# Moving PSUM additions, weight steps, turned weights and one projection in a chained attention and RWKV kernel

## The chip, the cores and the metric

The kernel runs on one core of a Trainium2 chip. The metric is the device time of one execution in microseconds (us). The engines are TensorE (PE), VectorE (DVE), ScalarE (ACT), GpSimd (POOL) and SyncE (SP), which issues the DMAs.

## The reference

Input `x` has 8 sequences of 112 tokens with 512 channels; the context `ctx` has 8 sequences of 375 tokens with 512 channels. All is float32. Four layers follow one another:

```python
x = x + alpha * softmax(x@w_q.T @ (ctx@w_k.T).T / sqrt(512)) @ (ctx@w_v.T) @ w_o.T     # L0
for layer in (L1, L2):                                  # RWKV, state taken from ctx
    xa = layer_norm(x);  sx = shifted(xa) - xa
    m  = tanh((xa + sx*maa_x) @ maa_w1) @ maa_w2        # five mixes w, k, v, r, g
    xw, xk, xv, xr, xg = xa + sx * (maa + m)
    w = exp(-exp(time_decay + tanh(xw@d1) @ d2))
    r, k, v, g = xr@Wr.T, xk@Wk.T, xv@Wv.T, silu(xg@Wg.T)
    for t in range(112):                                # 32 heads, states of 16 x 16
        a = k[t][:, None] * v[t][None, :]
        y[t] = r[t] @ (u*a + s);  s = a + w[t][:, None] * s
    x  = x + (group_norm(y) * g) @ Wo.T
    xc = layer_norm(x);  sxc = shifted(xc) - xc
    x  = x + sigmoid((xc+sxc*fr)@Wfr.T) * (square(relu((xc+sxc*fk)@Wfk.T)) @ Wfv.T)
for i in (1, 2):                                        # L3, 16 heads of 128
    q, k, v = norm(x)@wq+bq, ctx@wk+bk, ctx@wv+bv       # and one bias row for k and v
    x = x + softmax(q @ k.T / sqrt(128)) @ v @ wo + bo
x = x + gelu(norm(x) @ w_fc1 + b_fc1) @ w_fc2 + b_fc2
```

## The kernel before

**Layout.** Channels lie on the 128 partitions in 4 chunks (`NC`); tokens lie along the free axis, 896 in all, mostly handled in two halves (`h`) of 448.

**A generator beside the layers.** The values of both attentions of L3, and a few of its keys, do not depend on `x`. The generator `values()` makes them while the RWKV layers run. Each `fill(n)` in a layer's code takes it n products on. Its work is 51 units: four sets of weights with 12 units of values (`wv`) each, and a last one with 3 units of keys (`wk`). A unit is a block product in the manner of Strassen with seven products, `k1, k6, k7, k2, k8` and, one product each into the next unit's time, `k5` and `k9` (`last_two`, L893). A product of values is two matmuls of 128x512 (four records in the trace), and an engine then empties the PSUM bank; two banks, `mm0` and `mm1`, take turns. ACT copies `k1`, `k6`, `k7` (L956) and `k8` (L973). For `k2`, ACT copies (L966) and GpSimd adds to an earlier result in SBUF (L967). For `k5` and `k9`, DVE adds from PSUM (L898, L902). A finished tile is stored to DRAM (`store`) on SP's queue; context tiles `cv` come on the same queue, four ahead.

**Weights between sets.** The seven weight tiles of a set are sums of raw weights. `relay` changes them one at a time: it yields the name of the product after which the next step may run, and `after(what)`, called behind each product, runs it. A step is a DMA (`raw`) on SP or a sum on GpSimd (L814 and its neighbours). This runs at 490 to 520 us, 1115 to 1150 and 1342 to 1362. The change from the second to the third set loads all anew (`weights`) in the first channel mix.

**A RWKV layer** first turns its weights `Wg` and `Wv` to another order of columns: for each of the 16 tiles of 128x128, ACT copies it out (L407) and GpSimd copies it back in the new order (L408), by a buffer of two. Of the first layer this happens in L0, of the second in the first layer's channel mix. Then for each half `h`, `mixes` makes the five mixes (DVE adds the two-input products to `sx`, L447, and `xa`, L450; GpSimd does it for three of the five), with `fill(fills[4 + c])` after each chunk c. While `mixes(1, ...)` runs, `fill` takes the pieces of `projections(0, ...)`, so its numbers say how many of these pieces come between which chunks. A piece of projection r is 16 matmuls.

**Time mix.** Per layer, 64 steps in an order written out by hand (`manual_schedule`): `kv` = `vp` times `k` on DVE (L675, result in PSUM), one product of values, ACT copies the next step's `vp` into PSUM (`led`, L576 and L577) from `vj`, which a DMA has broadcast; DVE scans `decay` and `kv` to `st` (L679); GpSimd multiplies `st` by `r` to `rs` (L683, six buffers); a second product of values in 14 of 16 steps; and TensorE sums four `rs` at a time once six are waiting. Pieces of the group norm of the chunk before stand at the end of steps: among them a square on ACT and reciprocals on DVE (L609).

**The rest.** The channel mix scales on DVE (`xk`, `xr`, L725) the differences `sxc` that GpSimd makes (L350, L351). The attentions of L3 run from 1513 us on.

Of the kernel before, what the change touches and what calls it, by code (L numbers as in the profile page):

```python
# [29 lines left out]
P = 128  # L30
# [59 lines left out]
def turned(ap):  # L90

    return ap.rearrange("p (h q r) -> p q h r", h=HB, q=4)
# [16 lines left out]
def tile_kernel(ctx: ExitStack, tc: tile.TileContext, d: dict, out: bass.AP):  # L109
# [21 lines left out]

    ident = const.tile([P, P], F32, name="ident")
    make_identity(nc, ident)
    mean_c = const.tile([P, P], F32, name="mean_c")
# [81 lines left out]
    def layer0():  # L216
# [3 lines left out]
        with (  # L220
# [3 lines left out]
            tc.tile_pool(name="a0s", bufs=2, space=PSUM) as ps2,  # L224
        ):
            w_q, w_k = weight("L0_xattn_w_q"), weight("L0_xattn_w_k")
            nc.sync.dma_start(x, d["xT"])
# [143 lines left out]
    def time_mix_inputs(n, pre, names, ones_t, first, k, v, r, g, decay, rows):  # L371
# [7 lines left out]
        with (  # L379
# [22 lines left out]
            for f in "gv":  # L402
                for o in range(NC):
                    for c in range(NC):
                        w = ws[f][:, c, o * P : (o + 1) * P]
                        t = work.tile([P, NH], F32, tag="e", name=f"turn{f}{n}_{o}_{c}")[:, :P]
                        nc.scalar.copy(t, w)  # L407
                        nc.gpsimd.tensor_copy(w.rearrange("p (q h r) -> p q h r", q=4, h=HB), turned(t))  # L408

# [48 lines left out]
            def projections(h, xw, xg):  # L458

                p = mm(ps, f"ps_d{n}_{h}")[:, :NH]  # L460
                for c in range(NC):
                    nc.tensor.matmul(p, d1[:, c, :], xw[:, c, :], start=c == 0, stop=c == NC - 1)
                td = one.tile([P, NH], F32, tag="td", name=f"td{n}_{h}")
                nc.scalar.activation(td, p, AF.Tanh)
# [66 lines left out]
            values_filler, filler = filler, pieces  # L531
            following = projections(1, *mixes(1, (2, 1, 2, 1, 1, 0, 0, 0)))
            filler = values_filler
# [227 lines left out]
    def rwkv_layers():  # L761
        with tc.tile_pool(name="rc", bufs=1) as one:
# [5 lines left out]
            with tc.tile_pool(name="rs", bufs=1) as setup:  # L768
                heads = setup.tile([P, P + P + HS - 1], F32, name="heads")
                nc.sync.dma_start(heads, d["heads"])  # L770

                nc.vector.tensor_copy(ones_t.rearrange("p (q h r) -> p q h r", q=4, h=HB), turned(heads[:, :P]))
                same = setup.tile([P, P], F32, name="same")
                for q in range(4):
                    nc.sync.dma_start(same[32 * q : 32 * (q + 1)], turned_rows(d["heads"][:, :P], q))
                nc.scalar.mul(mean_h.rearrange("p (q h r) -> p q h r", q=4, h=HB), turned(same), 1.0 / HS)
                nc.vector.tensor_sub(less_mean_h, ident, mean_h)

                for r in range(4):
                    at = P + HS - 1 - 4 * r  # L780
                    nc.vector.tensor_copy(pick[:, r], heads[:, at : at + 16 * HB - 3 : 4])
# [6 lines left out]
    def values():  # L788
# [31 lines left out]
        def relay(at, old, new):  # L820
# [5 lines left out]
            for y, o, k in ((a11, 0, 0), (a21, 1, 0), (a22, 1, 1)):  # L826
                raw(y, at, o, k)
            yield "k1"
            nc.gpsimd.tensor_sub(old["k1"], a11, a21)
# [7 lines left out]
            raw(old["k8"], at, 1, 1)  # L837
            new.update(k1=a11, k6=old["k6"], k7=old["k1"], k2=old["k7"], k8=old["k8"], k5=old["k9"], k9=old["k2"])
            yield "k5"
# [41 lines left out]
        def store(y, u, o, j):  # L881
# [10 lines left out]
            else:  # L892
                nc.sync.dma_start(where[:, t], y)  # L893

        def last_two(u, f, u2, u3, s, at):
            p = bank(u, f, f"k5_{u}")
            product(p, block(at), s["k5"])
            nc.vector.tensor_add(u3, p, u3)  # L898
            store(u3, u, 1, 1)
            yield "k5"  # L900
            product(p, block(at + 2), s["k9"], start=False)
            nc.vector.tensor_add(u2, p, u2)  # L902
            store(u2, u, 0, 1)
            yield "k9"
# [11 lines left out]
        yield  # L916
        before, steps, following = iter(()), iter(()), None

        def after(what):
            nonlocal following  # L920
            if what == following:
                following = next(steps, None)
# [8 lines left out]
        for u, (at, unit) in enumerate(units):  # L931
# [9 lines left out]
            if unit == UNITS - 2 and at != 1:  # L941
                new = {}
                steps = relay(at + 1, s, new)
                ready = next(steps)
            elif unit == UNITS - 1 and at != 1:
                following = ready
            if unit % 3 == 0:
                for gr in groups:
# [14 lines left out]
            product(p, block(base + 5), s["k2"])  # L963

            y = shaped(pool.tile([P, C], F32, tag="k2", name=f"k2_{u}"), f)
            nc.scalar.copy(y, p)  # L966
            nc.gpsimd.tensor_add(p1, y, p1)  # L967
            store(p1, u, 0, 0)
# [114 lines left out]

    def attention(i, h_in, work, kv, ps, ps2, keep, mlp_norm):
        nonlocal filler
# [220 lines left out]
    def layer3():  # L1306
        with (
# [5 lines left out]
        ):  # L1313
            h_in = keep.tile([P, NC, N], F32, name="h_in")
            with tc.tile_pool(name="t3s", bufs=1, space=PSUM) as ps2:
                def mlp_norm(h, bank):
# [13 lines left out]
                for i in (1, 2):  # L1330
                    attention(i, h_in, work, kv, ps, ps2, keep, mlp_norm)
            mlp(h_in, work, ps, keep, shared["t_mlp"])
# [86 lines left out]
```

## Time and profile before

| quantity | us |
|---|---|
| median of 3 runs (lowest to highest) | 3005.23 (2998.66 to 3009.64) |
| the profiled execution, own time | 3006.6 |
| its span | 3004.8 |
| TensorE busy | 2874.8 |
| DVE busy | 1713.4 |
| ACT busy | 862.4 |
| GpSimd busy | 732.9 |
| first time mix | 364.5 to 631 |
| second time mix | 1003 to 1281 |
| attentions of L3 and MLP | 1513 to the end |

In rows of the profile the first item is the line of the kernel, then engine, operation, and tiles written and read. A count follows an x; then come the busy time in us, the mean ns of one, and the idle time before them with what ended it. In rows of waits the three numbers are the total us, how many times, and the longest. The granted clock of TensorE over the span is 0.981.

### The profile page before, as it was taken

To read this page: it belongs to the slowest core of one execution; us is meant where nothing else is said; L and a number is where in the kernel's file an instruction comes from. 1 tells how busy PE (TensorE), PEld (TensorE's weight loads), DVE (VectorE), ACT (ScalarE), POOL (GpSimd) and SP (SyncE) were. 2 spreads that over 40 slices of the span, in tenths; PEclk is the share of its full clock that TensorE was granted. 3 is DMA by queue.
4 is the path that set the end of the run, shared out by engine and by line. 5 is a ranking of instruction groups with operands and counts; after the bars stand their busy time and mean duration, and the time that the engine had idled before them with its cause. 6 is when DMAs were issued, how large, how long until landed. Compare 5 with 4: busy or idle time off the path is not lost.

```text
span 3004.8 us, 29759 instructions
## 1 busy us (share of the span) xinstructions
PE 2874.8 (96%) x10130; PEld 1571.3 (52%) x10130; DVE 1713.4 (57%) x2588; ACT 862.4 (29%) x1750; POOL 732.9 (24%) x636
## 2 busy tenths in 40 slices
PE   8989999998999998999899999999899999999999
PEld 4734443343444433346456666656465666656544
DVE  1464198956343588844366555646755565646455
ACT  2123354423243344422132122212221221212311
POOL 3142057534221366632200101020001001010030
PEclk9989999999999999999999999999999999999999
DMA  7421398843311788744225252434243433432110
GB/s 252 148 88 45 122 291 264 250 129 118 95 62 55 223 240 264 229 137 132 85 87 169 90 165 96 138 105 145 70 128 106 138 117 121 139 102 90 45 57 25
DMA packets 199319, 402.91 MB, mean 134 GB/s; under 512 B 33288, under 2 KB 119592, under 8 KB 192384
## 3 DMA queue, kind: packets, MB, share of 16 engines
q1 hardware_dynamic: 199168, 401.01, 42.9%
q8 instruction: 81, 1.33, 0.2%
q14 instruction: 70, 0.57, 0.1%
HBM read 323.16 MB, written 77.91 MB: 133 GB/s over the span
## 4 chain that ended last, share of the span: by engine, by line
PE 50%; DVE 2%; ACT 1%; issue 1%; POOL 0%; DMA 0%; DVEq 0%; ACTq 0%; POOLq 0%
PE av L1214 6%; PE sc L1201 5%; PE ps_k1k L1017 5%; PE ps_k7k L1017 5%; PE ps_k5k L1017 5%; PE pt L1204 3%; PE ps_k6k L1017 2%; PE ps_k7q L1017 2%; PE ps_k5q L1017 2%; PE ps_k5o L1017 1%; PE ps_k1o L1017 1%; PE ps_k7o L1017 1%; PE ps_k1q L1017 1%; PE ps_k5fc L1017 1%; PE ps_k7fc L1017 1%; PE ps_k6q L1017 1%
## 5 line engine op out<-in xcount | busy, mean ns | idle before, releaser
L873 PE MATMUL ps_vk<-wv,cv 128*128 128x512 f32 x1336 | 613.8, 608 | 49.7 <-DVE k L902 12.2
L873 PEld LDWEIGHTS ps_vk<-wv,cv 128*128 128x128 f32 x1336 | 250.8, 193 | 393.1 <-issue 300.9
L210 ACT ACTIVATE prob<-sc,top 112x376 f32<-112x376 f32 (+1 forms) x264 | 152.1, 576 | 712.2 <-DVE top L207 590.9
L683 POOL TENSOR_TENSOR rs<-st,r 128x896 f32<-128x896 f32 x128 | 246.9, 1929 | 281.1 <-DVE st L679 164.1
L679 DVE TENSOR_TENSOR_SCAN st<-decay,kv 128x904 f32<-128x904 f32 x128 | 260.3, 2034 | 9.1
L1201 PE MATMUL sc<-k,q 128*112 128x376 f32 x512 | 200.7, 485 | 1.0 <-ACT prob L210 0.8
L1214 PEld LDWEIGHTS av<-pts,v 125*128 125x128 f32 (+1 forms) x1536 | 184.8, 193 | 29.9 <-DVE pts L1210 15.1
L1214 PE MATMUL av<-pts,v 125*128 125x112 f32 (+1 forms) x1536 | 188.2, 277 | 0.9 <-DMA v<-wvs 0.9
L1194 POOL COPY k<-over_k 128x4 f32<-128x4 f32 x64 | 15.9, 253 | 679.3 <-PE sc L1201 611.0
L1017 PE MATMUL ps_k1k<-cx,w_L_xattn_wk 128*128 128x375 f32 x480 | 177.8, 483 | 1.6 <-ACT rstdk L1035 1.5
L207 DVE TENSOR_REDUCE top<-sc 112x1 f32<-112x376 f32 (+1 forms) x264 | 143.6, 545 | 30.5 <-PE sc L1201 15.9
L956 ACT COPY k<-ps_vk 128x512 f32<-128x512 f32 (+1 forms) x153 | 89.2, 583 | 226.6 <-PE ps_vk L873 204.7
L675 DVE TENSOR_TENSOR kv<-vp,k 128x904 f32<-128x904 f32 x128 | 140.9, 1101 | 17.2 <-ACT vp L577 10.7
L1204 PEld LDWEIGHTS pt<-ident,prob 112*125 112x125 f32 (+1 forms) x768 | 98.2, 176 | 59.5 <-DVE prob L212 32.9
L212 DVE TENSOR_SCALAR prob<-prob,total 112x376 f32<-112x376 f32 (+1 forms) x264 | 118.9, 453 | 7.1
L1017 PEld LDWEIGHTS ps_k1k<-cx,w_L_xattn_wk 128*128 128x128 f32 x480 | 89.7, 192 | 59.7 <-issue 3.3
L1204 PE MATMUL pt<-ident,prob 112*125 112x112 f32 (+1 forms) x768 | 116.1, 272 | 1.9 <-DVE prob L212 1.9
L577 ACT COPY vp<-vj 128x896 f32<-128x896 f32 x124 | 112.8, 910 | 16.3 <-DMA vj<-rows 12.4
L967 POOL TENSOR_TENSOR k<-k,k 128x512 f32<-128x512 f32 (+1 forms) x51 | 65.9, 1292 | 200.3 <-ACT k L966 91.4
L1221 DVE TENSOR_TENSOR ctxt<-av,bv 128x448 f32<-128x448 f32 x64 | 40.0, 625 | 127.6 <-PE av L1214 127.6
L1201 PEld LDWEIGHTS sc<-k,q 128*112 128x112 f32 x512 | 78.8, 176 | 41.4 <-ACT prob L210 6.4
L1017 PE MATMUL ps_k7k<-cs,wsk 128*128 128x375 f32 x240 | 88.5, 480 | 0.6 <-DVE k L1122 0.6
(375 smaller groups left out, 4713.8 us busy)
## 6 DMA issues: line engine op xcount, KB each, us to landing
vj<-rows SPq DMA_DIRECT2D x124, 448.0 KB
cv<-blocks SPq DMA_DIRECT2D x181, 251.5 KB
cs<-blocks SPq DMA_DIRECT2D x120, 375.0 KB
wvs<-k SPq DMA_DIRECT2D x128, 256.0 KB
v<-wvs SPq DMA_DIRECT2D x64, 512.0 KB
cx<-in_ctxT SPq DMA_DIRECT2D x38, 750.0 KB
v<-wvs SPq DMA_DIRECT2D x64, 252.0 KB
wvs<-k SPq DMA_DIRECT2D x64, 224.0 KB
```

The lines of the kernel that those rows point to most:

```text
L207: nc.vector.tensor_reduce(top, scores, AX.X, ALU.max, negate=True)
L210: nc.scalar.activation(prob, scores, AF.Exp, bias=top, accum_out=total)
L212: nc.vector.tensor_scalar(prob, prob, total, None, ALU.mult)
L577: nc.scalar.copy(vp[:, :, 1:], by_batch(vjs.pop((c, j))))
L675: nc.vector.tensor_mul(flat(kv), flat(vp), flat(k[:, c]))
L679: nc.vector.tensor_tensor_scan(flat(st), flat(decay[:, c]), flat(kv), 0.0, ALU.mult, ALU.add)
L683: nc.gpsimd.tensor_mul(by_batch(rs), st[:, :, :L], by_batch(r[:, c, :]))
L873: nc.tensor.matmul(to, left, right, start=start and n == 0, stop=k == 1, skip_group_check=True)
L1017: nc.tensor.matmul(to, lhsT, rhs, start=start and k == 0, stop=k == 1, skip_group_check=not start)
L1201: nc.tensor.matmul(sc, q[:, o, tok], kt[:, o, :], start=True, stop=True)
L1204: nc.tensor.transpose(pt[t][:nt, o, :], prob[:, t0 : t0 + nt], ident[:L, :L])
L1214: nc.tensor.matmul(av[:, o, :], v[:nt, t, o * HD : (o + 1) * HD], pts[:nt, t, o, :], start=t == 0, stop=t == 2,)
```

## The change

It has five parts. (1) `k5` and `k9` are emptied as `k2` is: a copy by ACT into a tile of tag `k2`, now with two buffers, and an addition by GpSimd. (2) `relay`'s steps run two products later than the one they name. (3) `Wg` and `Wv` are turned by halves of 128x1024, four ACT copies and four DVE copies per layer. (4) In `mixes(1, ...)` a sixth number goes from 0 to 1: a piece of the projections of half 0 (that of r) comes between chunks 1 and 2. (5) The identity matrix is made in three places, each in a pool of its own, and `td` shares a buffer with `t4`.

```diff
@@ -129,8 +129,11 @@
 
     x = xpool.tile([P, NC, N], F32, name="x")
 
-    ident = const.tile([P, P], F32, name="ident")
-    make_identity(nc, ident)
+    def identity(pool, name):
+        ident = pool.tile([P, P], F32, name=f"ident_{name}")
+        make_identity(nc, ident)
+        return ident
+
     mean_c = const.tile([P, P], F32, name="mean_c")
     nc.vector.memset(mean_c, 1.0 / C)
     eps = const.tile([P, 1], F32, name="eps")
@@ -223,6 +226,7 @@
             tc.tile_pool(name="a0p", bufs=2, space=PSUM) as ps,
             tc.tile_pool(name="a0s", bufs=2, space=PSUM) as ps2,
         ):
+            ident = identity(keep, "a0")
             w_q, w_k = weight("L0_xattn_w_q"), weight("L0_xattn_w_k")
             nc.sync.dma_start(x, d["xT"])
             cxs = {}
@@ -400,12 +404,15 @@
                 nc.sync.dma_start(d2[part], d[pre + names["d2"]])
             ws = {f: weight(f"{pre}W{f}") for f in "gvkr"}
             for f in "gv":
-                for o in range(NC):
-                    for c in range(NC):
-                        w = ws[f][:, c, o * P : (o + 1) * P]
-                        t = work.tile([P, NH], F32, tag="e", name=f"turn{f}{n}_{o}_{c}")[:, :P]
-                        nc.scalar.copy(t, w)
-                        nc.gpsimd.tensor_copy(w.rearrange("p (q h r) -> p q h r", q=4, h=HB), turned(t))
+                for half in range(2):
+                    w = ws[f][:, 2 * half : 2 * half + 2].rearrange("p c n -> p (c n)")
+                    t = work.tile([P, NC, NH], F32, tag="half", name=f"turn{f}{n}_{half}")
+                    t = t.rearrange("p c n -> p (c n)")[:, : 2 * C]
+                    nc.scalar.copy(t, w)
+                    nc.vector.tensor_copy(
+                        w.rearrange("p (a q h r) -> p a q h r", q=4, h=HB, r=4),
+                        t.rearrange("p (a h q r) -> p a q h r", q=4, h=HB, r=4),
+                    )
 
             def own_half(f, c, h):
 
@@ -460,7 +467,7 @@
                 p = mm(ps, f"ps_d{n}_{h}")[:, :NH]
                 for c in range(NC):
                     nc.tensor.matmul(p, d1[:, c, :], xw[:, c, :], start=c == 0, stop=c == NC - 1)
-                td = one.tile([P, NH], F32, tag="td", name=f"td{n}_{h}")
+                td = one.tile([P, NH], F32, tag="t4", name=f"td{n}_{h}")
                 nc.scalar.activation(td, p, AF.Tanh)
                 yield
 
@@ -529,7 +536,7 @@
 
             pieces = projections(0, *mixes(0, (2, 2, 4, 3, 2, 2, 2, 2) if n == 2 else (0, 0, 0, 3, 2, 2, 2, 2)))
             values_filler, filler = filler, pieces
-            following = projections(1, *mixes(1, (2, 1, 2, 1, 1, 0, 0, 0)))
+            following = projections(1, *mixes(1, (2, 1, 2, 1, 1, 1, 0, 0)))
             filler = values_filler
             for left in (pieces, following):
                 for _ in left:
@@ -774,7 +781,7 @@
                 for q in range(4):
                     nc.sync.dma_start(same[32 * q : 32 * (q + 1)], turned_rows(d["heads"][:, :P], q))
                 nc.scalar.mul(mean_h.rearrange("p (q h r) -> p q h r", q=4, h=HB), turned(same), 1.0 / HS)
-                nc.vector.tensor_sub(less_mean_h, ident, mean_h)
+                nc.vector.tensor_sub(less_mean_h, identity(setup, "rs"), mean_h)
 
                 for r in range(4):
                     at = P + HS - 1 - 4 * r
@@ -825,6 +832,7 @@
             a11, a21, a22 = x1[:, :2], x1[:, 2:], x2[:, :2]
             for y, o, k in ((a11, 0, 0), (a21, 1, 0), (a22, 1, 1)):
                 raw(y, at, o, k)
+            new.update(k1=a11, k6=old["k6"], k7=old["k1"], k2=old["k7"], k8=old["k8"], k5=old["k9"], k9=old["k2"])
             yield "k1"
             nc.gpsimd.tensor_sub(old["k1"], a11, a21)
             yield "k5"
@@ -835,7 +843,6 @@
             raw(old["k7"], at, 0, 1)
             yield "k8"
             raw(old["k8"], at, 1, 1)
-            new.update(k1=a11, k6=old["k6"], k7=old["k1"], k2=old["k7"], k8=old["k8"], k5=old["k9"], k9=old["k2"])
             yield "k5"
             raw(old["k5"], at, 0, 0)
             new["k1"] = old["k5"]
@@ -892,14 +899,20 @@
             else:
                 nc.sync.dma_start(where[:, t], y)
 
+        def add(y, p, u, f, what):
+
+            z = shaped(pool.tile([P, C], F32, tag="k2", name=f"{what}_{u}", bufs=2), f)
+            nc.scalar.copy(z, p)
+            nc.gpsimd.tensor_add(y, z, y)
+
         def last_two(u, f, u2, u3, s, at):
             p = bank(u, f, f"k5_{u}")
             product(p, block(at), s["k5"])
-            nc.vector.tensor_add(u3, p, u3)
+            add(u3, p, u, f, "k5")
             store(u3, u, 1, 1)
             yield "k5"
             product(p, block(at + 2), s["k9"], start=False)
-            nc.vector.tensor_add(u2, p, u2)
+            add(u2, p, u, f, "k9")
             store(u2, u, 0, 1)
             yield "k9"
 
@@ -914,11 +927,14 @@
             shared["over", i] = spill.tile([NG, C], F32, name=f"overs{i}")
             nc.sync.dma_start(shared["over", i], over)
         yield
-        before, steps, following = iter(()), iter(()), None
+        before, steps, following, made = iter(()), iter(()), None, []
 
         def after(what):
+
             nonlocal following
-            if what == following:
+            made.append(what)
+            while following in made[:-2]:
+                del made[: made.index(following) + 1]
                 following = next(steps, None)
 
         def late():
@@ -944,6 +960,7 @@
                 ready = next(steps)
             elif unit == UNITS - 1 and at != 1:
                 following = ready
+                made.clear()
             if unit % 3 == 0:
                 for gr in groups:
                     for b in (2 * (unit // 3), 2 * (unit // 3) + 1):
@@ -961,10 +978,7 @@
             p1, u2, u3 = kept
             p = bank(u + 1, f, f"k2_{u}")
             product(p, block(base + 5), s["k2"])
-
-            y = shaped(pool.tile([P, C], F32, tag="k2", name=f"k2_{u}"), f)
-            nc.scalar.copy(y, p)
-            nc.gpsimd.tensor_add(p1, y, p1)
+            add(p1, p, u, f, "k2")
             store(p1, u, 0, 0)
             after("k2")
             yield
@@ -1081,7 +1095,7 @@
 
         return put
 
-    def attention(i, h_in, work, kv, ps, ps2, keep, mlp_norm):
+    def attention(i, ident, h_in, work, kv, ps, ps2, keep, mlp_norm):
         nonlocal filler
         pre = "L3_xattn_"
         scale = 1.0 / math.sqrt(HD)
@@ -1312,6 +1326,7 @@
             tc.tile_pool(name="t3p", bufs=2, space=PSUM) as ps,
         ):
             h_in = keep.tile([P, NC, N], F32, name="h_in")
+            ident = identity(keep, "l3")
             with tc.tile_pool(name="t3s", bufs=1, space=PSUM) as ps2:
                 def mlp_norm(h, bank):
                     if not h:
@@ -1328,7 +1343,7 @@
                     )
 
                 for i in (1, 2):
-                    attention(i, h_in, work, kv, ps, ps2, keep, mlp_norm)
+                    attention(i, ident, h_in, work, kv, ps, ps2, keep, mlp_norm)
             mlp(h_in, work, ps, keep, shared["t_mlp"])
 
     shared["spill"] = ctx.enter_context(tc.tile_pool(name="spill", bufs=1, space=bass.MemoryType.DRAM))
```

## The prediction

> **What bounds the kernel now.** I read the page's busy table first, then the windows of each stage, then what TensorE waited for, and last the groups of the instructions that the change touches.
>
> ```profile
> PE 2874.8 (96%) x10130; PEld 1571.3 (52%) x10130; DVE 1713.4 (57%) x2588; ACT 862.4 (29%) x1750; POOL 732.9 (24%) x636
> ```
>
> TensorE is busy for 2874.8 of 3004.8 us, and the change takes no matmul away. All that can be won is the 130 us of TensorE idle time and what is lost where the granted clock is low. So I look for stages in which either lies (first two numbers: start and end, then length; then PE, PEld, DVE, ACT, POOL busy, PE clock, DMA share, GB/s).
>
> ```profile
> 200.00:345.00 145.00, 140.49 (x381) 64.72 (x381) 55.32 (x74) 51.07 (x72) 33.90 (x33) 0.94 0.16 55
> 364.50:631.00 266.50, 253.51 (x760) 102.41 (x761) 239.09 (x178) 129.44 (x241) 166.89 (x99) 0.99 0.88 261
> 713.00:802.00 89.00, 81.42 (x206) 40.00 (x206) 28.63 (x37) 18.35 (x49) 36.20 (x50) 0.94 0.18 56
> 1003.00:1281.00 278.00, 257.47 (x762) 102.82 (x763) 238.62 (x178) 131.01 (x241) 166.75 (x99) 0.99 0.85 248
> 1346.00:1394.00 48.00, 41.99 (x318) 38.47 (x317) 34.85 (x33) 16.81 (x26) 16.23 (x14) 0.93 0.51 162
> 1513.00:3005.00 1492.00, 1465.39 (x5801) 902.04 (x5799) 853.77 (x1745) 335.62 (x820) 162.62 (x173) 1.00 0.34 107
> ```
>
> The two time mixes (rows 2 and 4) lose 13 and 20.5 us of TensorE; there DVE is busy 239 us, 90% and 86%. The first layer's mixes and projections (row 1), its channel mix (row 3) and the second layer's channel mix (row 5) lose 4.5, 7.6 and 6 us, and run at 0.93 to 0.94 of the clock. The last row is half the kernel, and the change leaves its work as it is. What TensorE waits for, in the first time mix, then in the second:
>
> ```profile
> PE ps_vk L873 <- DVE k L902: 4.2, 2, 2.7
> PE ps_vk L873 <- DVE k L898: 3.7, 3, 2.2
> PE ps_vk L873 <- ACT k L973: 2.5, 2, 1.7
> ...
> PE ps_vk L873 <- DVE k L902: 5.5, 2, 2.7
> PE ps_vk L873 <- ACT k L966: 4.0, 2, 2.3
> PE ps_vk L873 <- ACT k L956: 3.0, 2, 2.0
> PE ps_vk L873 <- DMA wv<-in_L_xattn_wv: 2.6, 1, 2.6
> PE ps_vk L873 <- DVE k L898: 1.4, 4, 0.4
> ```
>
> The values' products have two PSUM banks. A bank whose emptying stands in DVE's queue behind a scan (2.03 us) or a group norm reciprocal (1.53 us) comes free late. That is 7.9 + 6.9 = 14.8 us by the DVE rows.
>
> **The additions.** Per unit of values the DVE additions of k5 and k9 from PSUM become an ACT copy and a GpSimd addition each, as k2 has it already:
>
> ```profile
> L683 POOL TENSOR_TENSOR rs<-st,r 128x896 f32<-128x896 f32 x128 | 246.9, 1929 | 281.1 <-DVE st L679 164.1 <-PE ps_vk L873 101.6 <-DMA vj<-rows 6.8
> L967 POOL TENSOR_TENSOR k<-k,k 128x512 f32<-128x512 f32 x48 | 62.2, 1295 | 182.3 <-ACT k L966 86.9 <-DMA cv<-blocks 78.4 <-PE ps_vk L873 13.1
> L902 DVE TENSOR_TENSOR k<-ps_vk,k 128x512 f32<-128x512 f32 x48 | 32.6, 679 | 15.8 <-PE ps_vk L873 15.6
> L966 ACT COPY k<-ps_vk 128x512 f32<-128x512 f32 x48 | 28.1, 585 | 39.9 <-PE ps_vk L873 39.0
> ```
>
> A time mix holds 35 of the 102 additions. DVE gives up 35 x 0.679 = 24 us (239 to 215), ACT takes 35 x 0.585 = 20 (129 to 150), GpSimd 35 x 1.295 = 45 (167 to 212, 80% of 266). No engine passes TensorE's 254. The new copies stand on ACT before the next `vp` copy (0.91 us), where DVE's addition stood before the scan. A bank now waits for 0.585 in place of 0.679 us, in the queue with more room. I take off the 14.8 us of DVE waits and put 2 back on ACT, whose own rows (9.5 us) stay: a group norm delays `kv`, then `vp`, then the copy behind it. Of the clock (0.99 over 544 us, some 5 us) half comes back: -2.5. The additions on GpSimd are waited for only by the stores to DRAM in SP's queue. Behind those stand the loads of `vj` and `cv`. `vj` lands 7 to 8 us after its issue and, by my reading of the trace, some 3 us before its use at the median; that is the cover, and the slower rival below is what happens without it. The shared tag has two buffers, about 7 us of time, so a copy rarely waits for GpSimd.
>
> Here a rule speaks against the change. First the rows:
>
> ```profile
> L679 DVE TENSOR_TENSOR_SCAN st<-decay,kv x128: 2025/2037/2040, 366.2 to 1278.7; 128x904 f32<-128x904 f32 x128
> ...
> L450 DVE TENSOR_TENSOR xw<-xw,xa x16: 610/990/1520, 199.0 to 923.2; 128x448 f32<-128x448 f32 x16
> ```
>
> (ns: least, median, most.) The scan keeps its 2025 to 2040 ns though some 115 of its 260 us lie beside GpSimd work; its `kv` is in PSUM, as is one input of L898, L902 and `kv`'s own product. So the time mixes lose nothing by contention. The mixes' addition has both inputs in SBUF: 610 ns alone, 380 more at the median. The Trainium skill, "SBUF — State Buffer", section "Who interferes with whom", says why: a DVE instruction with two SBUF inputs shares an interface with a GpSimd instruction that reads SBUF, and the second to start waits for the whole of the first. Of the 102 additions 12 fall into mixes and channel mixes. By the rule each blocks DVE for 1.295 us against the 0.679 that DVE saves: 12 x 0.62, 7 us lost. By the row each costs 0.38, so 12 x 0.30, 4 us are won. Much of either lies beside TensorE; I charge 2 us of loss, in the first channel mix, between the two.
>
> **Weight steps two products later.** A step's DMAs on SP and its GpSimd work are moved; none is added. A product takes 1.72 us, so each is 3.4 us later. SP no longer holds its queue for TensorE to be done with the old weights. But the raw weights have 3 to 5 products left before their use in place of 5 to 7, that is 5.2 to 8.6 us, and the three loads in the first time mix took 4.8 to 8.4 us from issue to last packet (issued 498.4, 506.8, 510.3; landed 506.9, 511.6, 516.2), those of the second 6 to 8. The weight waits in the second are 2.6 us by the row above, and 1.9 more. Between zero and 6 us of new waiting per time mix, I take 2.5 each: +5. GpSimd has about 34 us of work in the 27 us of such a change of weights, so it falls some 5 us behind; six `rs` buffers and two `st` buffers take that up.
>
> **Turned weights.** 64 copies of 128x128 on ACT, each with a turning copy on GpSimd, become per layer four copies of 128x1024 on ACT and four on DVE.
>
> ```profile
> L408 POOL COPY w_L_xattn_Wg_None<-turng 128x128 f32<-128x128 f32 x32 | 11.9, 403 | 1.9 <-ACT turng L407 1.7
> PE ps_vk L873 <- ACT k L973: 7.0, 1, 7.0
> 719.80:730.10 10.30, 5.90 (x8) 2.61 (x9) 6.54 (x10) 4.08 (x14) 9.84 (x17) 0.50 0.49 140
> ```
>
> In the first channel mix ACT stands in front of a values copy, waiting for GpSimd to turn its last tile, and TensorE stands still for 7.03 us; then it runs at 0.50. That is 7.03 and half of 5.9, 10 us. A long ACT copy is estimated at 1.02 us from the 583 ns of 512 and 910 of 896 elements, a DVE copy at 1.23 from 679 for 512 and 1101 for 904: about 4.5 on ACT, 5 on DVE, spread, and no longer tied tile by tile. 10 less the 2 charged above: -8 (-3 to -10). In the first attention the same loop held a query's copy for 4.5 us (the wait of `ps_tv` on ACT `q`); it may turn into a wait for the context's loads: -4 (0 to -5).
>
> **One projection between mixes.** In 276 to 300 us the clock is 0.79, in 919 to 931 0.72: 5 and 3.4 us lost, while DVE makes the mixes. The r projection of the other half, 16 matmuls and some 12 us, moves into this stretch. It doesn't change what DVE does, except that two small instructions come earlier. The window of the first layer holds 4.5 idle and 8.7 of clock. I take -4 and -2 (together 0 to -12), half of the loss, since the projection comes after only the second of four chunks.
>
> The Trainium skill, "TensorE: Matmul & The Clock Gate", section "What's actually happening", lets the clock drop after an idle window of 3.4 us. The largest gap in 276 to 300 is 0.7 us, and the clock still fell to 0.79. By the rule a gap that short costs only itself and this part would be worth 1 us; by the row 6. I take the row.
>
> **Waits on DVE elsewhere.** At 825 us TensorE waits 2.2 us for the addition of L902, clock 0.79 in the 8 us around it; at 1385 5.3 us for that of L898, which stands behind a row of channel mix instructions, clock 0.76 over 10. That is 3.9 and 7.7 us; part goes to GpSimd beside DVE, so -3 (0 to -4) and -6 (0 to -8).
>
> The identity, made three times (under 1 us of GpSimd each), is covered by other loads at its places, at most 2 us if not. The last attentions: 0, within 2.
>
> Sum: time mixes -14.8 + 2 - 2.5 + 5 = -10; channel mix 1 -8; first attention -4; projection -6; waits elsewhere -9. Together -37. The profiled execution took 3006.6 us, 1.4 above the median of 3005.2 of runs that spread over 11; so 2969.6, said as **2969 us**.
>
> **The rivals.** (A) GpSimd makes the stores late, and these the loads. Each added addition waits for an `rs` (1.93) and takes 1.3; if SP stands for it, `vj` eats its 3 us and `vp`, `kv`, scan and all behind come late. For: GpSimd goes from 63 to 80%, DMA share 0.88. Against: today's k2 additions do the same to their store, and the `vj` waits before ACT come to 12.4 us in all. With 70 additions at 0.5 us each the gain is gone; at 0.9 us it is +63 against -37, near **3033**. (B) The stalls only change queue: a copy behind `vp` is as late as an addition behind a scan. The time mixes give 0 and the rest -27: **2980**. (C) The weights come late, 8 us more per time mix, and the projection and the first attention give nothing: -37 + 16 + 10 = -11, **2996**. (D) The added GpSimd work doesn't bind and DVE's freedom takes the other waits along: time mixes -25, **2954**.
>
> **How the numbers follow.** My forecast 0.50, D 0.10, B 0.18, C 0.10, A 0.12. About 0.5%, 15 us, is what a measurement of this kernel tells from no change. Forecast, D and most of B lie below 2990: 0.77; C and the edge of B are within: 0.11; A above: 0.12. The range 2942 to 3008 takes in D and C with the bounds of the parts, and leaves out most of A.
>
> **What would show it.** Right: no PE wait on a DVE `k` in the time mixes and DVE near 215 us; no gap of 7 us in the first channel mix; clock near 1 in the first layer's second mixes; GpSimd near 212 us with `st` still at 2.03. Wrong: `vp` waiting for `vj`, stores late behind GpSimd; new `ps_vk` waits on `wv` loads; scan or `kv` longer than before; time mixes longer than 266 and 278 us.

## The result, and the profile after

The changed kernel takes 2979.31 us (median of 4 runs, 2978.26 to 2983.53), the kernel before, on the same chip, 3007.43: a ratio of 0.9912 with a 95% interval of 0.9885 to 0.9938. That is 28 us less; 38 were forecast against this median, 37 by the sum. The profiled execution took 2979.44 us, its span is 2977.4.

The page's busy times, and the windows of the two time mixes and of the second half's mixes in the first layer:

```profile
PE 2858.6 (96%) x10130; PEld 1564.0 (53%) x10130; DVE 1684.0 (57%) x2494; ACT 907.6 (30%) x1796; POOL 847.3 (28%) x678
...
276.00:308.00 32.00, 30.46 (x85) 13.76 (x84) 20.32 (x30) 4.79 (x9) 11.67 (x10) 0.89 0.07 25
369.70:626.60 256.90, 247.24 (x750) 100.78 (x748) 219.68 (x142) 147.34 (x272) 207.43 (x132) 1.00 0.90 266
990.40:1254.20 263.80, 250.53 (x750) 101.60 (x748) 219.78 (x142) 147.02 (x272) 207.73 (x132) 0.99 0.88 258
```

DVE has 220 us of work in a time mix (239 before), ACT 147, GpSimd 207. What TensorE waits for in the two:

```profile
PE ps_vk L880 <- ACT k L973: 3.6, 3, 1.7
PE ps_vk L880 <- POOL wv L841: 2.7, 1, 2.7
PE ps_gm L602 <- ACT gsq L603: 1.9, 3, 0.6
PE ps_vk L880 <- ACT k L987: 1.4, 1, 1.4
...
PE ps_vk L880 <- DMA wv<-in_L_xattn_wv: 3.2, 2, 2.2
PE ps_vk L880 <- ACT k L905: 3.2, 2, 1.8
PE ps_vk L880 <- POOL wv L841: 2.2, 1, 2.2
```

No wait on a DVE `k` is left. New are the waits on GpSimd's weight sum (L841, 2.35 us long). A third view is needed to see why: what DVE waited for in the first time mix, before (two lines) and after (two), then how long ACT waited for `kv` there, before and after:

```profile
DVE k L898 <- PE ps_vk L873: 10.2, 6, 5.4
DVE k L902 <- PE ps_vk L873: 5.0, 4, 2.0
...
DVE kv L682 <- ACT vp L584: 24.9, 34, 3.8
DVE st L686 <- POOL rs L690: 3.0, 2, 1.6
...
ACT vp L576 <- DVE kv L675: 44.0, 32, 3.5
...
ACT vp L583 <- DVE kv L682: 17.7, 24, 2.8
```

Before, DVE stood at an addition until its product was done, 15.2 us, and ACT's copy into the next `vp` waited 44.0 us in all for DVE's `kv`, which reads the `vp` before. After, DVE waits mostly for the next `vp` (and 3.0 us for GpSimd to free a buffer): it has room, and ACT's wait is down to 17.7 us.

The gap of 7 us in the first channel mix is gone too. From 705 to 730 us this is all that TensorE waits for:

```profile
PE ps_fk L161 <- DVE xk L732: 2.5, 1, 2.5
```

To see where the time went I compare the same matmul in two traces, that is, how much earlier it starts. Stage by stage, in us (negative: won by the change; the last two columns say what a stage loses again when one part is undone, from the profiles of two experiments below):

| stage, by the time before | change | additions undone | turning undone |
|---|---|---|---|
| first attention, to 158 | +2.0 | -0.8 | -3.2 |
| layer 1, inputs and first half, to 272 | +1.9 | -2.3 | +0.3 |
| layer 1, second half, to 354 | +0.1 | -0.7 | 0 |
| first time mix, to 633 | -7.5 | +4.4 | +0.7 |
| to the first channel mix, 714 | +1.1 | -1.1 | 0 |
| first channel mix, to 810 | -8.2 | +6.3 | +11.7 |
| layer 2, inputs and first half, to 905 | -7.2 | +5.5 | +1.6 |
| layer 2, second half, to 998 | +3.3 | -2.4 | -2.5 |
| second time mix, to 1283 | -12.1 | +11.3 | -0.7 |
| to the middle of the second channel mix, 1414 | -2.9 | +2.9 | 0 |
| the rest | +2.0 | +1.6 | +1.9 |
| all | -27.5 | +24.6 | +9.7 |

The first row scatters: kernels with the same first attention differ by up to 4 us from one profile to the next. DVE's waits there for the context's DMAs differ too, from 9.9 to 12.8 us; that they are the cause is not shown. The last row, where the change leaves the work as it is, scatters as much, from 0.7 won to 4.6 lost. So a few us of one profile carry no weight by themselves.

### The profile page after: what moved, and what is told of

Its sections match the earlier page's. It is cut to its first block, busy times and chain, and to the rows that moved or that the text cites. A ratio compares the mean times of both kernels' runs of the same rounds, so it can differ in the third digit from the quotient of the medians.

```text
span 2977.4 us, 29803 instructions
## 1 busy us (share of the span) xinstructions
PE 2858.6 (96%) x10130; PEld 1564.0 (53%) x10130; DVE 1684.0 (57%) x2494; ACT 907.6 (30%) x1796; POOL 847.3 (28%) x678
## 4 chain that ended last, share of the span: by engine, by line
PE 80%; DVE 8%; POOL 4%; issue 3%; ACT 2%; DMA 2%; SPq 0%; DVEq 0%; POOLq 0%; ACTq 0%
PE ps_vk L880 13%; PE av L1228 6%; PE sc L1215 5%; PE ps_k1k L1031 5%; PE ps_k7k L1031 5%; PE ps_k5k L1031 5%; PE ps_o L161 3%; PE pt L1218 3%; PE ps_k6k L1031 3%; PE ps_k7q L1031 2%; PE ps_fk L161 2%; DVE st L686 2%; PE ps_r L479 2%; PE ps_k L479 2%; PE ps_k5q L1031 2%
## 5 line engine op out<-in xcount | busy, mean ns | idle before, releaser
L880 PE MATMUL ps_vk<-wv,cv 128*128 128x512 f32 x1336 | 602.2, 602 | 31.1 <-DMA wv<-in_L_xattn_wv 11.6
L906 POOL TENSOR_TENSOR k<-k,k 128x512 f32<-128x512 f32 (+1 forms) x153 | 201.6, 1318 | 308.7 <-ACT k L905 260.1
L905 ACT COPY k<-ps_vk 128x512 f32<-128x512 f32 (+1 forms) x153 | 89.2, 583 | 181.0 <-PE ps_vk L880 179.1
L973 ACT COPY k<-ps_vk 128x512 f32<-128x512 f32 (+1 forms) x153 | 89.0, 582 | 154.2 <-PE ps_vk L880 147.6
L1218 PEld LDWEIGHTS pt<-ident_l,prob 112*125 112x125 f32 (+1 forms) x768 | 97.8, 176 | 61.8 <-DVE prob L215 36.2
L1218 PE MATMUL pt<-ident_l,prob 112*125 112x112 f32 (+1 forms) x768 | 116.6, 273 | 2.9 <-DVE prob L215 2.8
```

Of the source, the lines that this page charges most:

```text
L880: nc.tensor.matmul(to, left, right, start=start and n == 0, stop=k == 1, skip_group_check=True)
L906: nc.gpsimd.tensor_add(y, z, y)
L1218: nc.tensor.transpose(pt[t][:nt, o, :], prob[:, t0 : t0 + nt], ident[:L, :L])
```

## The experiments

All are compared with the changed kernel's 2979.3 us; ratios are to the kernel before, run beside them.

**1. The additions undone.**

```diff
-            add(u3, p, u, f, "k5")
+            nc.vector.tensor_add(u3, p, u3)
-            add(u2, p, u, f, "k9")
+            nc.vector.tensor_add(u2, p, u2)
```

> The changed kernel with k5 and k9 added by DVE from PSUM again, all else changed. Theory 1 (the freed DVE queue made the gain): the time mixes go back to about 264 and 269 us from 256.9 and 263.7, the second channel mix loses its 5.5 us and the inputs of the second layer about 6, so +25 us on 2979, near 3004. Theory 2 (the gain of the time mixes came from weight steps that no longer hold SP's queue): +10 or less, near 2988, time mixes within 3 us of the changed kernel's.

3003.7 us, ratio 0.9987 (0.9980 to 0.9995). Theory 1 holds: nearly the whole gain goes with the additions, and the old waits are back to the tenth in the first time mix. In the first channel mix the wait behind the turning tiles is replaced by one behind DVE (last line):

```profile
PE ps_vk L880 <- DVE k L915: 4.2, 2, 2.7
PE ps_vk L880 <- DVE k L911: 3.7, 3, 2.2
...
PE ps_vk L880 <- DVE k L911: 5.8, 1, 5.8
```

**2. The delay of the weight steps undone.**

```diff
-            while following in made[:-2]:
+            while following in made[: len(made) - 0]:
```

> The changed kernel with every weight step at once behind its product, as before. Theory 1: the delay costs more than it brings (waits on DMA wv and on GpSimd's wv of 2.7 in the first and 5.4 us in the second time mix), so -4 us, near 2975, with these waits gone. Theory 2 (the delay frees SP and GpSimd at the right time): +10, near 2989, and vp waits longer for vj. Theory 3, GpSimd now carries the additions and an immediate step puts its sums ahead of them: between 0 and +6.

2974.2 us, 0.9889 (0.9872 to 0.9906): this and the changed kernel's interval overlap. In the profile 3.3 of its 5 us are gone before 190 us, where nothing of the step has run. From there it wins 1.7 us in all, and that behind 1414 us, where no step runs any more. In the first time mix it loses 3.6 where the steps run, in the second it wins 2.4. In the first, this wait takes the place of the 2.7 us on GpSimd:

```profile
PE ps_gm L602 <- ACT gsq L603: 4.0, 1, 4.0
```

So the delay is worth nothing that can be measured; theory 2 is out, and between 1 and 3 the runs do not decide. In the second time mix the new wait on GpSimd's weight sum goes with the delay.

**3. The turning undone.** The loop of 16 tiles with ACT and GpSimd stands in place of the two halves.

> The changed kernel with Wg and Wv turned tile by tile by ACT and GpSimd. Theory 1 (by comparing the two traces): the first channel mix loses 7 us again and the first attention wins 2, so +5, near 2984. Rival: both places lose, as forecast, +12, near 2991. Second rival: with the additions on GpSimd too, the tiles wait longer for GpSimd than before, and the gap of 7 us in the channel mix becomes 9 or more.

2986.2 us, 0.9921 (0.9905 to 0.9938). TensorE in the first channel mix:

```profile
PE ps_vk L877 <- ACT k L984: 4.2, 1, 4.2
PE ps_fk L161 <- DVE xk L729: 3.7, 2, 2.5
PE ps_vk L877 <- ACT k L902: 3.0, 1, 3.0
```

The second rival is right on the sum: undoing costs 11.7 us in this stage, more than the 8.2 that the whole change wins there. Two of three waits are on ACT copies again, one of them the new copy of an addition. So the two parts need each other here: with either undone, 6.3 or 11.7 us are lost. In the first attention undoing wins 3.2 us, within the scatter of that row. The wait on `ACT q` that was to go did go, but another came in the changed kernel:

```profile
PE av L338 <- DVE pts L334: 4.3, 1, 4.3
PE ps_w_vo L294 <- ACT w_vo L297: 3.3, 1, 3.3
```

ACT's first copy of `Wv` waits for its DMA until 63.27 us, and the copy of `w_vo` stands behind it (3.3); later `pts` waits behind a copy of context that isn't there yet (3.1 before, 4.3 after).

**4. The projection undone.**

```diff
-            following = projections(1, *mixes(1, (2, 1, 2, 1, 1, 1, 0, 0)))
+            following = projections(1, *mixes(1, (2, 1, 2, 1, 1, 0, 0, 0)))
```

> The changed kernel with the r projection of half 0 back behind all chunks. Theory 1 (the two traces): nothing in the first layer (the stretch only moved), 3.3 us won in the second, so -3, near 2976. Rival, the forecast: the projection fills idle and slow TensorE time, so undoing it costs +6, near 2985. What is to be seen in either: the clock from 276 to 308 us, and what TensorE waits for at ruk.

2976.9 us, 0.9896 (0.9878 to 0.9913), which overlaps with the changed kernel's interval. In the profile the second half of layer 1 gains 1.3 us, that of layer 2 2.3, but the two time mixes lose 1.5 and 2.7 of it again; why is not shown. So the projection costs time in its own stages, and over the kernel nothing that these runs can tell. The same window as in the changed kernel, then what TensorE waits for in the changed kernel's two second halves:

```profile
276.00:308.00 32.00, 30.99 (x80) 15.30 (x80) 18.09 (x27) 4.66 (x8) 9.86 (x9) 0.89 0.00 1
...
PE ps_ruk L533 <- DVE ruk L524: 1.1, 2, 0.6
PE ps_ruk L533 <- DVE ruk L524: 2.3, 1, 2.3
```

The clock is 0.89 in either. In the changed kernel TensorE runs the projection at full speed from 278 to 290 us, and DVE is busy for only 4.1 of these 12 us, since the matmuls that feed the next chunks stand behind the projection. Then the slow stretch begins as before, 12 us later, and `ruk` now waits behind the mixes in DVE's queue.

**5. ACT empties the bank, DVE adds.**

```diff
-            nc.gpsimd.tensor_add(y, z, y)
+            (nc.gpsimd if what == "k2" else nc.vector).tensor_add(y, z, y)
```

> The changed kernel, but behind ACT's copy of k5 and k9 DVE adds (from SBUF) in place of GpSimd; k2's addition stays on GpSimd. DVE keeps the work that the kernel before gave it, GpSimd gets none of the new work, and the bank is freed by ACT. Theory 1a (the gain is that the bank is emptied in ACT's queue, not in DVE's): most of it stays, +3 to +6 us on 2979, no PE wait on a DVE k in the time mixes. Theory 1b (the gain is DVE's lower load, 239 to 220 us in a time mix): it is lost, +20 or more, near 3000, with DVE back near 238 us. Where both inputs are in SBUF beside GpSimd, the addition should take more than 679 ns in some places.

3012.7 us, 1.0017 (1.0008 to 1.0025): by 0.2% slower than before the change, though no bank waits for DVE. The first time mix (waits of TensorE, then of DVE), DVE's new addition (ns: least, median, most), and two places at which it met GpSimd (start and length in us):

```profile
PE ps_vk L880 <- ACT k L973: 9.0, 5, 2.6
PE ps_vk L880 <- ACT k L987: 4.9, 2, 2.5
...
DVE k L906 <- ACT k L905: 16.5, 11, 4.5
...
L906 DVE TENSOR_TENSOR k<-k,k x102: 615/693/2392, 204.2 to 1403.3; 128x512 f32<-128x512 f32 x96, 128x500 f32<-128x500 f32 x6
...
413.27 1.93 POOL L690 TENSOR_TENSOR rs<-st,r 128x896 f32<-128x896 f32 x1 [1.43 <-DVE st L686]
414.24 1.50 DVE L906 TENSOR_TENSOR k<-k,k 128x512 f32<-128x512 f32 x1
...
1287.22 1.92 POOL L690 TENSOR_TENSOR rs<-st,r 128x896 f32<-128x896 f32 x1 [0.57 <-DVE st L686]
1287.29 2.39 DVE L906 TENSOR_TENSOR k<-k,k 128x512 f32<-128x512 f32 x1 [0.22 <-ACT k L905]
```

Theory 1a does not hold: a bank that comes free early is not enough. The waits on a DVE `k` turn into waits on ACT, whose copies stand behind a `vp` that waits for a late `kv` (57.9 us in this time mix, 17.7 in the changed kernel's). DVE still stands at the addition until ACT has copied, and with two inputs in SBUF the addition takes up to 2.39 us beside GpSimd: its mean over the 96 of full size is 979 ns, against 679 from PSUM. So DVE is busy 249 us of a time mix of 275, where the additions from PSUM (experiment 1) left it at 237: besides the bank, this run also changes DVE's load, so it does not weigh the two apart. Experiment 6 comes nearer.

In both places shown, DVE's addition ends 0.54 us after the end of the GpSimd instruction that was running when it began. This holds throughout. Of the 102 additions, 38 began with more than 0.15 us of a GpSimd instruction still to run, and every one of them ended 0.545 to 0.552 us after that instruction; the other 64 took 0.615 to 0.695 us.

**6. DVE's load put back, without its wait.**

```diff
             nc.gpsimd.tensor_add(y, z, y)
+            if what != "k2":
+                nc.vector.reciprocal(idle, idle)
+                nc.vector.reciprocal(idle, idle)
```

> The changed kernel, and in DVE's queue, where k5's and k9's additions stood before, two reciprocals of 128x48 on a scratch tile: some 0.76 us of DVE work by the row of 128x224 (1526 ns), waiting for nothing. So DVE has the work of the kernel before, but doesn't wait for the end of a product. Theory W (the waiting counted: DVE stood 15.2 and 23.4 us in the time mixes for the products of k5 and k9): at most +8, near 2985. Theory L (the load counted): +20 or more, near 3000.

2997.8 us, 0.9971 (0.9961 to 0.9981): +18.5. One of the two reciprocals, and the first time mix:

```profile
L910 DVE RECIPROCAL idle<-idle x102: 426/443/454, 1.1 to 1285.5; 128x48 f32<-128x48 f32 x102
...
366.90:636.92 270.02, 254.82 (x756) 102.33 (x754) 246.37 (x220) 148.44 (x273) 208.49 (x132) 0.98 0.88 257
```

The reciprocals took 0.43 to 0.45 us each, 0.9 in place of 0.76, so the load is 31 us per time mix, some 7 over that of the additions (DVE is busy 246 us in the first one, against 237 with them). Even so, theory L is the nearer: work that waits for nothing costs most of what the DVE additions cost. Theory W's +8 is out. It speaks against theory 1a of experiment 5, too: here ACT empties the banks, DVE stands at no addition, and most of the gain is gone. As the load was a third too large, the runs don't say which share is the wait's.

**7. More work on GpSimd.** Behind each added addition one more GpSimd instruction on the scratch tile.

```diff
             nc.gpsimd.tensor_add(y, z, y)
+            if what != "k2":
+                nc.gpsimd.tensor_add(z, z, z)
```

> The changed kernel with one more GpSimd addition of the same size behind each of k5's and k9's, on the scratch tile, its result not used further: 102 x 1.3 us more, 35 of them in each time mix, so GpSimd would go from 207 to about 253 of 257 us there. Rival A of the forecast (GpSimd binds, stores and loads come late): +30 or more, near 3010 and above, with rs late, st waiting for rs, vp waiting for vj. Theory 1 (GpSimd still has room in the changed kernel, and six rs and two scratch buffers take up the rest): below +12. In between: the reserve was some tenths of a us per addition.

3002.2 us, 0.9985 (0.9977 to 0.9993): +23. Each took 1.10 us in place of 1.3. Window and waits of the first time mix:

```profile
365.20:628.60 263.40, 249.39 (x750) 101.71 (x748) 219.66 (x142) 147.07 (x272) 240.36 (x166) 0.99 0.88 259
...
PE ps_vk L880 <- POOL wv L841: 6.1, 1, 6.1
...
DVE st L686 <- POOL rs L690: 6.7, 4, 3.3
```

This is in between: 102 instructions cost 0.2 us each, no more, but not nothing. It comes back first where weights change (the sum on GpSimd now holds TensorE for 6.1 us), then in `st`, which waits for a free buffer. `vp` waits for `vj` 6.1 us in all, 2.8 in the changed kernel: too little for rival A, by which the loads run late.

**8. The additions left out.** The kernel copies k5 and k9 and adds them nowhere.

```diff
-            nc.gpsimd.tensor_add(y, z, y)
+            if what == "k2":
+                nc.gpsimd.tensor_add(y, z, y)
```

> The changed kernel with the additions of k5 and k9 left out altogether (so part of the values is not computed): ACT copies, nothing adds, GpSimd goes back from 207 to about 163 us in a time mix. Theory G0 (GpSimd's additions are hidden): 2976 to 2980. Theory G1 (they cost part of what DVE's relief brings, by weight sums on GpSimd that come late, waits of 2.7 and 2.2 us, and rs): -5 to -10, near 2971, with the waits on GpSimd's wv gone.

2956.7 us, 0.9835 (0.9822 to 0.9847): -22.6. The two time mixes, by DVE's first and last scan, and a wait of TensorE in the second:

```profile
361.03:614.33 253.30, 246.91 (x750) 100.77 (x748) 219.78 (x142) 147.46 (x272) 166.66 (x98) 1.00 0.92 272
975.68:1236.44 260.76, 248.73 (x750) 101.28 (x748) 219.78 (x142) 147.16 (x272) 166.23 (x98) 0.99 0.89 260
...
PE ps_vk L880 <- POOL wv L841: 2.2, 1, 2.2
```

They are 3.6 and 3.0 us shorter than with the additions, and 3.0 of either is won where the weights change. The wait on GpSimd's weight sum is gone in the first, but still there in the second: there G1 is wrong, and the delay alone brings the wait (it goes in experiment 2). 4.8 of the 22.6 us come before 190 us, where no addition has run, and 2.5 behind 1414 us, where none runs any more. The rest lies in small pieces: 3.4 in the first layer's inputs, 1.5 before the first channel mix, some 2 in the second. So what GpSimd takes on is not free: 15 to 18 us, more than G1 gave. With the additions go also the stores' waits for them, so this is not the price of GpSimd's time alone. What DVE's relief is worth without this price is then, as an estimate, 24 + 15 to 18, some 40 us.

**9. The additions alone.** Experiments 2, 3 and 4 in one kernel.

> Of the whole change only the additions (and the buffers that they need): weight steps at once, weights turned tile by tile, projection at its old place. If the parts add up: 2986 (turning undone) less some 3 for delay and projection, near 2983; the first channel mix has the 9 us wait behind the turning copies. Rival: without the delay GpSimd can't keep up with weight steps and tiles, near 2995.

2988.9 us, 0.9939 (0.9926 to 0.9952). This is 6 above what adding up gave, and not the rival's 2995. Of the 11 us over the changed kernel's profile, 10.3 are in the first channel mix, by the same waits as in experiment 3.

**10. The projection one chunk later.**

```diff
-            following = projections(1, *mixes(1, (2, 1, 2, 1, 1, 1, 0, 0)))
+            following = projections(1, *mixes(1, (2, 1, 2, 1, 1, 0, 1, 0)))
```

> The changed kernel with the r projection of half 0 one chunk later, between chunks 2 and 3. Theory (DVE runs dry while TensorE does the projection, since the matmuls of the next chunks stand behind it, so placing only moves the slow stretch): no change, 2976 to 2982, clock from 276 to 308 us near 0.89. Rival (the projection was one chunk too early): -3 to -5, clock 0.95 or more.

2982.3 us, 0.9914 (0.9895 to 0.9934): no change. The same window as in the changed kernel:

```profile
276.00:308.00 32.00, 30.37 (x86) 13.51 (x86) 21.18 (x31) 3.94 (x8) 11.69 (x10) 0.95 0.07 22
```

The clock did rise, from 0.89 to 0.95, which the theory had not expected, and yet the stage is only 0.5 us shorter. TensorE is idle for 1.6 us here and for 1.5 in the changed kernel, so it is not waiting that took the rest; what did is not shown.

**11. Combined.** The delay and the projection undone as in experiments 2 and 4 (not shown again), the first layer's turning copies both on DVE.

```diff
-                    nc.scalar.copy(t, w)
+                    (nc.vector.tensor_copy if n == 1 else nc.scalar.copy)(t, w)
```

> Additions and turning as in the changed kernel, but the weight steps at once behind their products, the projection back behind all chunks, and for the first layer both turning copies on DVE (ACT no longer waits for Wv's DMA ahead of the copy that TensorE needs; that wait was 3.3 us). Theory: -2 -1 -3, near 2973, if the first attention isn't held by the context's DMAs anyway; rival (it is): near 2976.

2972.7 us, 0.9888 (0.9871 to 0.9905). The first attention ends 9.7 us earlier than in the changed kernel's profile, 6 earlier than in most others; the 3.3 us wait is gone. Some 3 of it are given back later. Of the kernels that compute everything it is the fastest here, with that of experiment 12, by 7 us against the changed kernel, whose interval it overlaps.

**12. Values between the mixes.** The combined kernel, in which after seven pieces `fill` in the second half's mixes takes products of values.

```diff
-            values_filler, filler = filler, pieces
-            following = projections(1, *mixes(1, (2, 1, 2, 1, 1, 0, 0, 0)))
+            values_filler = filler
+
+            def either():
+                for _ in range(7):
+                    next(pieces, None)
+                    yield
+                while True:
+                    next(values_filler, None)
+                    yield
+
+            filler = either()
+            following = projections(1, *mixes(1, (2, 1, 2, 1, 1, 2, 2, 2)))
```

> The combined kernel (2972.7), and two products of values after each of the last three chunks of the second half's mixes, where TensorE otherwise waits for DVE and the clock falls to 0.89. Theory: the idle and slow time of both layers there is filled, -5 to -8, near 2966. Rival: the products only move, the bank of the values and GpSimd's additions contend with the mixes' DVE instructions, and later stages lack these products: 2970 to 2976.

2972.4 us, 0.9885 (0.9873 to 0.9898), as without. The two stretches in the combined kernel, in this one, and a wait before the first channel mix in this one:

```profile
265.00:300.00 35.00, 34.57 (x92) 16.87 (x92) 20.60 (x31) 4.84 (x9) 10.38 (x9) 0.85 0.03 11
875.00:920.00 45.00, 44.38 (x126) 21.36 (x125) 23.96 (x36) 5.39 (x10) 15.48 (x13) 0.92 0.10 38
...
265.00:300.00 35.00, 35.00 (x108) 15.40 (x107) 20.12 (x31) 7.76 (x14) 14.51 (x12) 1.00 0.17 51
880.00:925.00 45.00, 44.60 (x139) 19.82 (x139) 25.35 (x33) 11.94 (x20) 21.92 (x22) 1.00 0.19 65
...
PE ps_vk L890 <- POOL wv L833: 8.7, 1, 8.7
```

Here the slow stretch is really filled: the clock is 1.00. But with twelve products done earlier, the sets of values change elsewhere, and the weights that are loaded anew now come 8.7 us late. In the middle of the second channel mix this kernel leads the combined one by only 0.8 us: what the early products save is lost again in between. This wait is the longest single loss that the profile shows there; the rest is not traced.

## Why the prediction was right, point by point

The forecast was 2969, 10 us too low; sign, range and the main mechanism held. Its terms did less well than its sum, and that the sum came so near is in part luck: the time mixes brought 10 us more than forecast, the projection and the first attention together 15 less.

- **Time mixes: -10, measured -19.6** (7.5 and 12.1). The waits on DVE went, as forecast, and no engine became the bound. The term was too small, since it counted only TensorE's waits that the profile puts down to DVE. DVE's work and its standing for products also made `kv`, and by it `vp` and ACT's copies, late. This is what the prediction's rival D says, and its -25 is nearer than the -10. "The queue with more room" was not the reason: with DVE loaded again most of the gain went, though ACT still emptied the banks (experiment 6; experiment 5 points the same way).
- **GpSimd's additions: 0 but for 2 us of contention, measured 15 to 18** (experiment 8). The forecast hid them behind buffers. It had foreseen that GpSimd falls behind while weights change (by 5 us; its own 34 us of work in 27 make 7), and took the buffers to be enough.
- **The delay of the weight steps: +5.** The forecast put the price on late DMAs. These came to 3.2 us in the second time mix, 2.6 before; what was new is GpSimd's sum, 2.7 and 2.2 us. Undoing the delay took the waits on GpSimd away and left 2.5 us on DMAs, yet it won nothing that can be told from the scatter (experiment 2).
- **Rival A** did not come, and its point of decision was not reached: an instruction on GpSimd cost 0.2 us per addition, not 0.5. Its chain wasn't seen either: `vj` came in time.
- **Contention.** For the time mixes the row was read rightly: the scan stayed at 2.04 us, though 195 of its 261 us in the changed kernel lie beside GpSimd work. For instructions with both inputs in SBUF the forecast set the rule that it cites, read as 1.295 us for each, against the row, 0.38, and took something between. Rule and row do not differ. As experiment 5 shows, the second does wait for the first to end, but that is only what is left of the first: next to nothing for 64 of 102 additions, up to 1.78 us for the others, 0.36 at the mean of all. The mixes' addition in the row (610 to 1520 ns) is such a mixture too. The charge of 2 us was small against what DVE lost: counted by the same mark, its instructions with two SBUF inputs were held up for 59 us in the first 1500 us of the changed kernel, 39 before, and 41 with the additions left out. How much of it reached TensorE is not shown.
- **First channel mix: -8, measured -8.2,** but both the turning and the additions are needed for it.
- **First attention: -4, measured +2,** and from +1.5 to -2.0 in other profiles with the same first attention. The step had named the place ("a wait for the context's loads"); besides, ACT now waits for `Wv`'s DMA in front of `w_vo`.
- **The projection: -6, measured +3.4** in its two stages, and nothing that can be told over the kernel (experiment 4). This step failed. It took matmuls put into a stretch for time filled. The projection runs while DVE is idle, and the slow stretch follows it. To fill it, work must be had beside DVE's mixes, as in experiment 12. The weighing of the clock is not refuted by this: the clock does fall without a long gap (to 0.85 in the combined kernel's stretch, with 0.43 us of idle time in 35), and is 1.00 once the stretch is full (experiment 12).
- **Waits elsewhere: -9, measured** -7.2 at the second layer's inputs and -5.5 at the second channel mix, of which 2.6 were lost again just before it. The row "to the middle" shows the difference.

## What to carry to other kernels

In a hand-ordered pipeline an instruction that waits for another engine's end costs its engine's work, its wait and all that stands behind it; the profile's waits of the bounding engine show only part of this (here 14.8 us of waits for a part that was worth 24). Before work goes to an engine that seems idle, ask for that engine's worst stretch, not its mean: here GpSimd was at 63% of the first time mix, and 3.0 of the 3.6 us that its additions cost there came where it also had weights to add. Work put into a slow stretch fills it only if it runs at the same time as what makes the stretch slow, and what it then displaces elsewhere must be counted too.

## What the runs showed of the hardware that I had not expected

The plainest is in experiment 5: a DVE addition with two SBUF inputs that begins while GpSimd works ends about 0.55 us after the GpSimd instruction does, however much of it is left. So its cost is set by the instant at which it begins, and a mean over many such additions hides this.

DVE's turning copy of 128x1024 from SBUF to SBUF took 0.69 us, as much as its addition of half that size from PSUM and much less than the 1.23 us that I had estimated:

```profile
L412 DVE COPY w_L_xattn_Wg_None<-turng x4: 680/689/777, 47.3 to 735.2; 128x1024 f32<-128x1024 f32 x4
```

ACT's copy of the same size took 1.05 us. A reciprocal of 48 columns took 0.44 us, where one of 224 took 1.53: about 6 ns a column and 0.15 fixed.
